# A two-layer graph attention kernel: one quarter of the attention weights read from its mirrored quarter

## The chip, the cores and the metric

The kernel runs on one core of a Trainium2 chip. A core has five engines that run side by side, each with its own queue in program order: TensorE (PE, matrix products), VectorE (DVE), ScalarE (ACT), GpSimd (POOL) and SyncE (SP, which here issues almost all transfers). Sixteen DMA engines move data between the core's memory SBUF and DRAM. The metric is the device time of one execution in microseconds (us), as the median of several runs; lower is better.

## The reference, cut to what matters

The input is 16 graphs (batches) of 1024 nodes with 256 features, and a symmetric 0/1 adjacency matrix with ones on its diagonal. Two layers follow each other. Layer 0 is attention with 8 heads of 32 features and an MLP; layer 1 is a single-head graph attention. The change touches the attention of layer 0:

```
normed = layer_norm(x, gamma1, beta1)
qkv    = normed.reshape(b_, n_, H, HD).transpose(0, 2, 1, 3)
scores = einsum('bhqd,bhkd->bhqk', qkv, qkv) * scale
masked = where(adj > 0, scores, -inf)
attn   = softmax(masked, axis=-1)
out    = einsum('bhqk,bhkd->bhqd', attn, qkv)
x      = x + out
y      = layer_norm(x, gamma2, beta2)
x      = x + gelu(y @ W1 + b1) @ W2 + b2
```

Queries, keys and values are the same matrix, and the mask is symmetric, so before the division by the row sum the weight of query q on key k equals that of query k on key q.

## The kernel before, in words

`fast_path` builds one straight program for all 16 batches. (A second path, `general_path`, runs only if a bound checked at the end is broken; it does not run here.)

*Attention of a batch* (`attention`, L966). The 8 heads make two groups `g` of four; the 1024 queries make two halves `qh` of 512; the keys make eight tiles `kt` of 128. A unit is one (qh, g, kt), 32 in a batch. `scores` (L971) lets PE form the scores of four heads in two PSUM tiles (L987), lets DVE add the mask to each (L1000, one 128x1024 instruction for two heads), and lets ACT take the exponential of each head with a running sum over the queries (L1007). Since weights are symmetric, that sum over the queries of a half is one half of a row sum. `weigh` (L1017) then multiplies the values with the weights into one PSUM tile of 128x512 for the group and half (L1022), one unit later: `go_on` (L1062) stands after the scores of the next unit. When a tile is complete it is copied (L1031), turned by PE and scaled by the inverted row sums (`finish`, L951; `invert`, L1038), and added to the layer's input by POOL (L964).

*The dense work of a batch* (`rest`, L1100) is the MLP and layer 1, cut into pieces of about 1.75 us of PE: `expand` (ph, L1158), `contract` (po, L1179), then projections and the attention of layer 1 (`weights`, lg, L1252, with DVE steps L1267 and L1272; `attend`, pa, L1291). It runs one batch behind the attention: while batch b does its attention, the pieces of batch b-1 fill PE between the units.

*Masks.* `turn_masks` (L889) loads four tiles of the adjacency matrix, converts them on DVE (L592) and transposes them by DMA; `compare_masks` (L909) checks on POOL (L917) and DVE (L924) that the mask is symmetric. `prologue` (L774) loads and normalises the next batch's input, with POOL forming the values (L814, L815).

*The order of the work* is set when the program is built. Each stream (attention, dense work, masks, next batch's prologue and so on, L1421 to L1483) yields a place on a common axis on which batch b's attention reaches from b to b+1; a loop (L1487) always advances the stream that is furthest behind. Beside this runs a clock of planned PE time (`clock`); `defer` (L757) puts an instruction into the queues once that clock has advanced by a given number of us. What results is one fixed order on each engine. Buffers come from pools of a fixed number; an engine waits in its queue until the buffer and the inputs of its next instruction are ready.

Pools that the change touches: `mqp` (converted masks, 2 buffers), `midp` (hidden layers and layer-1 matrices, 3), `ep` (exponentials, 6), `denp` (row sums).

Of the kernel before, what the change touches and what calls it, by code (L numbers as in the profile page):

```python
# [495 lines left out]
def fast_path(  # L496
# [49 lines left out]
    mqp = pool("mqp", 2)  # L546
# [3 lines left out]
    midp = pool("midp", 3)  # L550
    ep = pool("ep", 6)
# [222 lines left out]
    def prologue(b, st):  # L774
# [61 lines left out]
        if b == 0:  # L836

            tiles = [midp.tile([P, 2, N], I32, tag="mid", name=f"adj_0_{i}") for i in range(2)]
            adjs = [tiles[t // 2][:, t % 2] for t in range(TPH)]
            mqs = st["mq", 0] = mqp.tile([P, TPH, N], FP8, tag="mq", name="mq_0_0")  # L840
            m = st[0] = mkp.tile([P, NT // 2, QW, 2], FP8, tag="mk", name="mk_0_0")
            pairs = m.rearrange("p m q r -> p m (q r)").bitcast(BF16)

            def fetch(t):
                nc.sync.dma_start(adjs[t], rows(adj, 0, t))

            def convert(t):
                nc.vector.tensor_scalar(
                    mqs[:, t], adjs[t], 0.0, NEG8, op0=ALU.is_le, op1=ALU.mult, saturate=False
                )  # L850
                nc.sync.dma_start_transpose(pairs[:, :, t * P : (t + 1) * P], mqs[:, t].bitcast(BF16))

            for f, i in ((load, 0), (fetch, 0), (load, 1), (fetch, 1), (fetch, 2), (fetch, 3), (load, 2), (load, 3)):
                f(i)
            measure(0, "a")
            measure(1, "a")
            rectify(0)
            convert(0)
            rectify(1)
            measure(0, "b")  # L860
            convert(1)
            measure(1, "b")
            value(0)
            turn(0)
            convert(2)
            value(1)
            turn(1)
            convert(3)
            for f in (lambda i: measure(i, "a"), rectify):
                for i in (2, 3):  # L870
                    f(i)
            yield
            measure(2, "b")
            value(2)
            yield
            measure(3, "b")
            value(3)
            yield
            for i in (2, 3):
                turns.append((1, lambda i=i: turn(i)))  # L880
                yield
            return
# [83 lines left out]
    def attention(b, st):  # L966
        va, kT = st["va"], st["kT"]
        den = denp.tile([P, NQH, NT, H], F32, tag="den", name=f"den_{b}")


        def scores(qh, g, kt):  # L971
# [24 lines left out]
            for i in range(2):  # L996
# [7 lines left out]
                def weights(e=e, masked=masked, i=i):  # L1004
                    for j in range(2):
                        n = g * GH + 2 * i + j
                        nc.scalar.activation(  # L1007
                            e[:, j], masked[:, j], AF.Exp, scale=SCALE, accum_out=den[:, qh, kt, n : n + 1]
                        )
# [4 lines left out]

        acc, os, rl = {}, {}, {}

        def weigh(qh, g, kt, es):  # L1017
            if kt == 0:
                acc[g, qh] = pso.tile([P, QW], F32, tag="o", name=f"o_{b}_{g}_{qh}")
            o = acc[g, qh]  # L1020
            for j in range(GH):
# [4 lines left out]
                    start=(kt == 0),  # L1026
                    stop=(kt == NT - 1),
                )
            if kt == NT - 1:
# [8 lines left out]
        def invert(qh, g):  # L1038
            r = smallp.tile([P, TPH, GH], F32, tag="rl", name=f"rl_{b}_{g}_{qh}")
            ts, hs_ = slice(qh * TPH, (qh + 1) * TPH), slice(g * GH, (g + 1) * GH)  # L1040

            def f():
                nc.vector.tensor_tensor(r, den[:, 0, ts, hs_], den[:, 1, ts, hs_], op=ALU.add)
                nc.vector.reciprocal(r, r)

            rl[g, qh] = r, defer(2.5, f)

        units = [(qh, g, kt) for qh in range(NQH) for g in range(NG) for kt in range(NT)]
        for u in units:
# [4 lines left out]
            scored.append((weigh, (*u, es)))  # L1054
            qh, g, kt = u
            if qh == NQH - 1 and kt % TPH == TPH - 1:
                invert(kt // TPH, g)
                if kt < NT - 1:
                    close(kt // TPH, g)
            yield  # L1060
# [39 lines left out]
    def rest(b, st, tails):  # L1100
# [55 lines left out]
        def expand(c):  # L1156
            yield from wait_for(turn, c)
            hid = midp.tile([P, FC, CW], F32, tag="mid", name=f"hid_{b}_{c}")  # L1158
# [190 lines left out]
        fT = st["fT"] = midp.tile([P, DC, N], F32, tag="mid", name=f"fT_{b}")  # L1349
# [5 lines left out]
        uT = midp.tile([P, DC, N], F32, tag="mid", name=f"uT_{b}")  # L1355
# [64 lines left out]

    def stream_a():  # L1421
        for b in range(B):
            yield from spread(attention(b, states[b]), 32, b, b + 1)
        yield from spread(close_attention(), 4, B, B + .1)

    def stream_b():
        for b in range(B):
            done = 0.0
            place = b + 0.99
            yield place  # L1430
            for us, others in states[b]["rest"]:
# [8 lines left out]
                elif others:  # L1440
                    place = max(place, b + 1 + done / B_US)
                yield place
        for us, _ in tails[B]():
            clock[0] += us
            yield B + 1

    def stream_p():
        for b in range(B):
            for c in range(2):
                yield b + 0.91 + 0.025 * c  # L1450
                prepare(b, states[b], c)
            yield b + 0.96
# [12 lines left out]
    def stream_m():  # L1465
        for b in range(B):
            for qh in range(b == 0, NQH):
                yield from spread(turn_masks(b, qh, states[b]), 5, b + 0.5 * qh - 0.27, b + 0.5 * qh - 0.07)

    def stream_k():  # L1470
        for b in range(B):
            for qh in range(NQH):
                yield from spread(
                    compare_masks(b, qh, states[b]), TPH * (qh + 1), b + 0.5 * qh + 0.02, b + 0.5 * qh + 0.2
                )
# [85 lines left out]
```

## Time and profile before

| what | value |
|---|---|
| three runs | 3424.79, 3426.13, 3426.3 us; median 3426.13 |
| profiled execution | 3422.06 us, of which the profile's span is 3420.3 us |
| busy: PE / DVE / ACT / POOL | 98% / 82% / 60% / 26% of the span |
| DMA engines, main queue | 15.8% busy, 137.56 MB |
| clock granted to PE | 0.999 |
| first batch's attention | up to about 141 us |
| attention of batches 1 to 15 | about 141 us to 3262 us, 208 to 211 us each |
| end, dense work of the last batch alone | about 3262 us to 3420 us |

The times of the table's last rows are read from the first mask addition of each batch. In the profile's lines "L1000" is a line of the kernel, "out<-in" are the program's names of tiles, "xN" the number of instructions; behind the bar stand the busy time in us, the mean of one in ns, and the idle time of the engine just before them with what ended it. PE's records count twice the matmuls that the code names: each matmul of these 4-byte numbers appears as two.

### The profile page before, as it was taken

To read this page: it belongs to the slowest core of one execution; us is meant where nothing else is said; L and a number is where in the kernel's file an instruction comes from. 1 tells how busy PE (TensorE), PEld (TensorE's weight loads), DVE (VectorE), ACT (ScalarE), POOL (GpSimd) and SP (SyncE) were. 2 spreads that over 40 slices of the span, in tenths; PEclk is the share of its full clock that TensorE was granted. 3 is DMA by queue.
4 is the path that set the end of the run, shared out by engine and by line. 5 is a ranking of instruction groups with operands and counts; after the bars stand their busy time and mean duration, and the time that the engine had idled before them with its cause. 6 is when DMAs were issued, how large, how long until landed. Compare 5 with 4: busy or idle time off the path is not lost. (4 is left out here: it accounts for less than half of the span.)

```text
span 3420.3 us, 114618 instructions
## 1 busy us (share of the span) xinstructions
PE 3356.2 (98%) x49790; PEld 1603.4 (47%) x49790; DVE 2799.1 (82%) x5427; ACT 2061.6 (60%) x5192; POOL 880.6 (26%) x1038
## 2 busy tenths in 40 slices
PE   6899999999999999999999999999999999999998
PEld 1244444444444444444444444444444444444477
DVE  6788888888888978888888887888879788897854
ACT  6665666656566565666656656666665655666532
POOL 3422232222323222232222312223222232321120
PEclk9999999999999999999999999999999999999999
DMA  4111202112011121111211112120211211111000
GB/s 135 45 39 40 57 17 54 39 47 56 20 46 39 48 54 34 40 31 48 54 39 48 25 50 45 42 56 18 52 39 48 55 26 40 39 48 42 8 19 14
DMA packets 157471, 145.22 MB, mean 42 GB/s; under 512 B 81056, under 2 KB 116256, under 8 KB 156960
## 3 DMA queue, kind: packets, MB, share of 16 engines
q1 hardware_dynamic: 156672, 137.56, 15.8%
q8 instruction: 392, 6.42, 0.8%
q14 instruction: 119, 0.97, 0.1%
q10 hardware_dynamic: 288, 0.26, 0.0%
HBM read 104.21 MB, written 16.78 MB: 35 GB/s over the span
## 5 line engine op out<-in xcount | busy, mean ns | idle before, releaser
L1007 ACT ACTIVATE e<-e 128x512 f32<-128x512 f32 x1984 | 1224.8, 619 | 960.5 <-DVE e L1000 958.1
L1000 DVE TENSOR_TENSOR e<-s,mk 128x1024 f32<-128x1024 f32 x992 | 1168.1, 1218 | 195.2 <-PE s L987 192.7
L987 PE MATMUL s<-kT 32*64 32x512 f32 x8192 | 579.5, 615 | 1.1 <-DVE e L1000 0.9
L1022 PE MATMUL o<-e,va 128*32 128x512 f32 x4096 | 557.5, 606 | 1.3 <-ACT e L1007 1.3
L572 PE MATMUL lg<-fT,uT 128*32 128x256 f32 x7680 | 454.1, 379 | 0.0
L572 PE MATMUL pa<-gw,e 128*32 128x258 f32 x7552 | 453.3, 380 | 0.0
L572 PE MATMUL ph<-yT,w 128*32 128x256 f32 x7808 | 451.0, 379 | 0.0
L572 PE MATMUL po<-w,hid 128*32 128x256 f32 x7680 | 438.9, 379 | 0.0
L1007 ACT ACTIVATION_READ_ACCUMULATOR e<-e 128x1 f32 x1984 | 371.2, 187 | 0.0
L572 PEld LDWEIGHTS ph<-yT,w 128*32 128x32 f32 x7808 | 255.5, 110 | 213.0 <-issue 55.7
L572 PEld LDWEIGHTS lg<-fT,uT 128*32 128x32 f32 x7680 | 257.3, 110 | 200.5 <-issue 43.3
L572 PEld LDWEIGHTS pa<-gw,e 128*32 128x32 f32 x7552 | 252.3, 110 | 206.6 <-issue 56.5
L572 PEld LDWEIGHTS po<-w,hid 128*32 128x32 f32 x7680 | 249.6, 110 | 209.6 <-issue 62.8
L1022 PEld LDWEIGHTS o<-e,va 128*32 128x32 f32 x4096 | 83.6, 108 | 424.6 <-issue 198.9
L1267 DVE SCALAR_TENSOR_TENSOR e<-lg,gw,mk 128x256 f32<-128x256 f32 x512 | 221.7, 474 | 64.2 <-PE lg L572 37.4
L1273 ACT ACTIVATE e<-e,shift 128x512 f32<-128x512 f32 x256 | 182.2, 715 | 141.5 <-DVE e L1272 103.8
L964 POOL TENSOR_TENSOR h<-h,ot 128x512 f32<-128x512 f32 x64 | 84.7, 1323 | 697.8 <-DVE ot L960 697.8
L917 POOL TENSOR_TENSOR odd<-mk,mq 128x512 bf16<-128x512 fp8e5 x192 | 233.3, 1216 | 100.2 <-DVE uneven L924 100.2
L1170 DVE TENSOR_TENSOR hid<-ph,b1c 128x512 f32<-128x512 f32 x256 | 173.6, 683 | 77.8 <-PE ph L572 67.8
L1272 DVE SCALAR_TENSOR_TENSOR e<-e 128x512 f32<-128x512 f32 x256 | 209.5, 818 | 8.8
L987 PEld LDWEIGHTS s<-kT 32*64 32x64 f32 x8192 | 122.7, 130 | 161.0 <-issue 105.0
L744 POOL TENSOR_TENSOR rs_c<-ve_c,mhalf 128x2 f32<-128x2 f32 x64 | 44.5, 695 | 477.4 <-DVE ve_c L742 378.1
(135 smaller groups left out, 3477.0 us busy)
## 6 DMA issues: line engine op xcount, KB each, us to landing
adj<-in_adj_dram SPq DMA_DIRECT2D x248, 256.0 KB, 3.6
h<-in_x_dram SPq DMA_DIRECT2D x64, 256.0 KB, 4.0
xb<-in_x_dram SPq DMA_DIRECT2D x128, 128.0 KB, 2.3
out_dram<-z SPq DMA_DIRECT2D x128, 128.0 KB, 1.7
adj<-in_adj_dram SPq DMA_DIRECT2D x4, 512.0 KB, 7.0
mk<-mq SPq DMA_TRANSPOSE x128, 3.8
w<-in_L_gnn_W_dram SPq DMA_DIRECT2D x2, 1024.0 KB, 8.7
wo<-in_L_gnn_W_dram SPq DMA_DIRECT2D x2, 256.0 KB, 9.8
```

Source lines behind the costliest of these rows:

```text
L572: nc.tensor.matmul(out[c : c + HD], lhsT[:, c : c + HD], rhs, start=start, stop=stop)
L744: nc.gpsimd.tensor_tensor(rs, ve, mhalf[:, :nt], op=ALU.pow)
L917: nc.gpsimd.tensor_tensor(odd.rearrange("p (u v x) -> p u v x", u=2, v=2), key.rearrange("p (u v x) -> p u v x", u=2, v=2), query.rearrang ...
L964: nc.gpsimd.tensor_add(ho, ho, ot.rearrange("p t j d -> p t (j d)"))
L987: nc.tensor.matmul(sc[j // 2][c : c + P // 2, j % 2, :], kT[r, g, kt * P + c : kt * P + c + P // 2], kT[r, g, qs], start=j >= by_pe, stop= ...
L1000: nc.vector.tensor_tensor(e, masked, mb, op=ALU.add)
L1007: nc.scalar.activation(e[:, j], masked[:, j], AF.Exp, scale=SCALE, accum_out=den[:, qh, kt, n : n + 1])
L1022: nc.tensor.matmul(o[j * HD : (j + 1) * HD, :], va[:, kt, (g * GH + j) * HD : (g * GH + j + 1) * HD], es[j // 2][:, j % 2, :], start=(kt = ...
L1170: nc.vector.tensor_tensor(hid[:, f0 : f0 + 2, :], ph, b1c[:, f0 : f0 + 2].unsqueeze(2).to_broadcast([P, 2, CW]), op=ALU.add,)
L1267: nc.vector.scalar_tensor_tensor(e[:, j, :], lg[:, j, :], gw[:, kt, D : D + 1], st[c // 2][:, kt // 2, qs, kt % 2], op0=ALU.add, op1=ALU.add,)
L1272: nc.vector.scalar_tensor_tensor(e, e, ALPHA, e, op0=ALU.mult, op1=ALU.max)
L1273: ready = defer(2.5, lambda: nc.scalar.activation(e, e, AF.Exp, bias=shift))
```

## The change

Batches 1 to 15 no longer compute the quarter of queries 512 to 1023 on keys 0 to 511 (qh 1, kt 0 to 3). Its weights are those of queries 0 to 511 on keys 512 to 1023 (qh 0, kt 4 to 7), mirrored. Batch 0 is as before, apart from its row sums' layout.

- The units of a batch are now 16 of the first half, keys 4, 0, 5, 1, 6, 2, 7, 3 for each group, and then 8 of the second half, keys 4 to 7 only.
- `mirror`, for each of the 8 units that are the source: when its exponentials are there, DVE turns them in blocks of 32x32 into one tile `x` (1 MB, one buffer), two instructions of 128x1024. Then SP issues four writes of 256 KB, one for each 32 partitions, to a scratch in DRAM, where the blocks' place stands for their new partitions.
- `fetch`, 16 a batch: SP issues a read of 512 KB from the scratch into one of the two halves of a tile `em`. The next fetch into a half waits until PE and POOL have read it.
- `weigh_mirrored`, 16 a batch, two in each of the 8 later units: four matmuls of 256 columns add to the same PSUM tile as the unit's own. POOL adds up the 8 blocks of two fetches to row sums in five additions; DVE reduces these to the inverse (in `invert`).
- The pools `mqp`, `midp` and `ep` give up buffers (2 to 1, 3 to one for each of three tags, 6 to 4) for the new tiles.
- The order is moved: units have widths (1 for the first 16, 1.15 for the last 8), the dense work of a batch starts at 1.08 batches behind in place of 0.99 and only when the first half of the queries is finished (now at the last unit), and masks are turned and compared at other places.

```diff
-    mqp = pool("mqp", 2)
+    mqp = pool("mqp", 1)
...
-    midp = pool("midp", 3)
-    ep = pool("ep", 6)
+    midp = pool("midp", 1)
+    ep = pool("ep", 4)
+    xp = pool("xp", 1)
+    dramp = pool("dramp", 2, space=bass.MemoryType.DRAM)
...
                         nc.scalar.activation(
-                            e[:, j], masked[:, j], AF.Exp, scale=SCALE, accum_out=den[:, qh, kt, n : n + 1]
+                            e[:, j], masked[:, j], AF.Exp, scale=SCALE,
+                            accum_out=sums[kt // TPH, g][:, n, kt % TPH, qh : qh + 1],
                         )
...
+        def mirror(g, kt, es):
+            x = xp.tile([P, NT // 2 * GH, GH, HD], F32, tag="x", name=f"x_{b}_{g}_{kt}")
+            if g not in blocks:
+                blocks[g] = dramp.tile([NT // 2 * GH, NT // 2 * GH, HD, P], F32, tag=f"blocks{g}", name=f"blocks_{b}_{g}")
+
+            def turn(i):
+                nc.vector.transpose(
+                    x[:, :, 2 * i : 2 * i + 2, :].rearrange("p c h j -> p h c j"),
+                    es[i].rearrange("p h (c i) -> p h c i", i=HD),
+                )
+
+            def write():
+                for a in range(GH):
+                    nc.sync.dma_start(
+                        blocks[g][(kt - TPH) * GH + a].rearrange("c i e -> i c e"),
+                        x[a * HD : (a + 1) * HD].rearrange("p c h j -> p c (h j)"),
+                    )
+
+            defer(1.5, lambda: turn(0))
+            defer(3.5, lambda: turn(1))
+            defer(5.5, write)
+
+        def fetch(k):
+            g, t, half = k // (2 * TPH), k // 2 % TPH, k % 2
+            if k == 0:
+                blocks["e"] = midp.tile([P, 2, 2 * GH, P], F32, tag="mid0", name=f"em_{b}")
+            nc.sync.dma_start(
+                blocks["e"][:, half],
+                blocks[g][half * 2 * GH : (half + 1) * 2 * GH, t * GH : (t + 1) * GH].rearrange(
+                    "k b i e -> (b i) k e"
+                ),
+            )
+
+        def weigh_mirrored(k):
+            g, t, half = k // (2 * TPH), k // 2 % TPH, k % 2
+            e = blocks["e"][:, half]
+            if t == half == 0:
+                acc[g, 1] = pso.tile([P, QW], F32, tag="o", name=f"o_{b}_{g}_1")
+            o = acc[g, 1]
+            for j in range(GH):
+                nc.tensor.matmul(
+                    o[j * HD : (j + 1) * HD, half * CW : (half + 1) * CW],
+                    va[:, t, (g * GH + j) * HD : (g * GH + j + 1) * HD],
+                    e[:, :, j * HD : (j + 1) * HD],
+                    start=t == half == 0,
+                    stop=False,
+                )
+            add = lambda out, p, q: nc.gpsimd.tensor_tensor(out, p, q, op=ALU.add)
+            if half == 0:
+                if t == 0:
+                    blocks["rows", g] = denp.tile([P, TPH, P], F32, tag="rows", bufs=1, name=f"rows_{b}_{g}")
+                blocks["part"] = denp.tile([P, GH, P], F32, tag="part", bufs=1, name=f"part_{b}_{g}_{t}")
+                add(blocks["part"], e[:, :GH], e[:, GH:])
+            else:
+                part = blocks["part"]
+                add(part, part, e[:, :GH])
+                add(part, part, e[:, GH:])
+                add(part[:, :2], part[:, :2], part[:, 2:])
+                add(blocks["rows", g][:, t], part[:, 0], part[:, 1])
+            clock[0] += 0.45
+            if k + 2 < 2 * TPH * NG:
+                defer(2.5 + 2.0 * half, lambda: fetch(k + 2))
+            if t == TPH - 1 and half == 1:
+                invert(0, g)
+                close(0, g)
...
+        keys = list(range(NT))
+        if mirrored:
+            keys = [kt for pair in zip(keys[TPH:], keys[:TPH]) for kt in pair]
+        units = [(0, g, kt) for g in range(NG) for kt in keys]
+        keys = list(range(TPH if mirrored else 0, NT))
+        units += [(1, g, kt) for g in range(NG) for kt in keys]
...
+            if qh == 0:
+                if kt >= TPH:
+                    mirror(g, kt, es)
+                if n == NG * NT - 1:
+                    defer(2.0, lambda: fetch(0))
+                    defer(2.2, lambda: fetch(1))
+                yield 1.0
+                continue
+            if last:
+                invert(1, g)
+            widths = (0.5, 0.4, 0.25) if first else (0.3, 0.5, 0.35)
+            yield widths[0]
+            weigh_mirrored(k)
+            yield widths[1]
+            weigh_mirrored(k + 1)
+            k += 2
+            yield widths[2]
...
+    def starts(b):
+        return b + (1.08 if b else 0.99)
...
-                    place = max(place, b + 1 + done / B_US)
+                    place = max(place, start + length * done / B_US)
```

## The prediction

> **What bounds the kernel now.** I read the busy table first, then the groups, then the TensorE (PE) timeline of a few units in a steady batch, then the busy times of one whole batch, and last the landing times of the transfers.
>
> ```profile
> span 3420.3 us, 114618 instructions
> PE 3356.2 (98%) x49790; PEld 1603.4 (47%) x49790; DVE 2799.1 (82%) x5427; ACT 2061.6 (60%) x5192; POOL 880.6 (26%) x1038
> ...
> L1007 ACT ACTIVATE e<-e 128x512 f32<-128x512 f32 x1984 | 1224.8, 619 | 960.5 <-DVE e L1000 958.1
> L1000 DVE TENSOR_TENSOR e<-s,mk 128x1024 f32<-128x1024 f32 x992 | 1168.1, 1218 | 195.2 <-PE s L987 192.7
> L987 PE MATMUL s<-kT 32*64 32x512 f32 x8192 | 579.5, 615 | 1.1 <-DVE e L1000 0.9
> L964 POOL TENSOR_TENSOR h<-h,ot 128x512 f32<-128x512 f32 x64 | 84.7, 1323 | 697.8 <-DVE ot L960 697.8
> L1272 DVE SCALAR_TENSOR_TENSOR e<-e 128x512 f32<-128x512 f32 x256 | 209.5, 818 | 8.8
> ```
>
> PE is busy 98% of the span and its matmul groups show next to no idle time in front of them (1.1 us for 8192 score matmuls). A busy PE need not be a full one, so the timeline:
>
> ```profile
> 1047.38 3.64 PE L572 MATMUL ph<-yT,w 128*32 128x256 f32 x64
> 1050.94 1.11 PE L987 MATMUL s<-kT 32*64 32x512 f32 x16
> 1051.99 1.06 PE L1022 MATMUL o<-e,va 128*32 128x512 f32 x8
> 1052.87 5.36 PE L572 MATMUL po<-w,hid 128*32 128x256 f32 x96
> 1058.16 0.66 PE L1219 MATMUL ptf<-ident,ft 128*128 128x128 f32 x4
> 1058.75 1.11 PE L987 MATMUL s<-kT 32*64 32x512 f32 x16
> ```
>
> Columns: start, length. From start to start the scores of a unit cost 1.05 us (1051.99 - 1050.94), its weighing 0.88, 32 records of the dense layers 1.77 (5.29 for 96), four transposes 0.59. Summed over the instructions of a batch (32 units, 288 groups of four quarter matmuls at 0.44, 8 at 0.87, 16 sets of transposes) this is 205 us; a steady batch takes 208.5:
>
> ```profile
> 1395.90:1604.40 208.50, 206.66 (x3188) 96.78 (x3184) 176.13 (x341) 129.01 (x325) 54.90 (x64) 1.00 0.16 43
> ```
>
> (length; PE, weight loads, VectorE (DVE), ScalarE (ACT), GpSimd (POOL) busy; granted clock; DMA share; GB/s). So PE bounds the 15 steady batches, with only 3.4 us of a batch not explained by its work. DVE, at 176 us (84%), is the next.
>
> **The change part by part.** Batch 0 keeps all units; batches 1 to 15 do 24 units instead of 32.
>
> *Removed.* 8 score sets a batch: 8 x 1.05 = 8.4 us of PE, on the path. With them 16 mask adds (16 x 1.218 = 19.5 us of DVE) and 32 exponentials with their accumulator reads (32 x 0.806 = 25.8 us of ACT). ACT waits 958 us for the adds already, so its share is worth nothing.
>
> *PE, exchanged.* 8 weigh sets of 512 columns (8 x 0.88 = 7.0) become 16 of 256 columns. In the tile shape of the dense layers, also 256 wide, four cost 0.44: 7.1 us. Their moving operand is read in runs of 32; no row shows that, the strided weights of the dense layers run at the same pace, and I take 0.
>
> *DVE, added.* 16 turns of 128x1024 replace the 16 adds. No row shows a turn. Rows bound it: 0.84 us by the rate of the mask conversion (420 ns for 512), 1.63 by the statistics (407 ns for 256); I take the add's 1.22, as many elements in one instruction, and the middle. So the batch sum is unchanged but for two reductions (about 0.68 each, as a 128x512 reduce), yet the place changes: all turns lie in the first 16 units. By the built order of the changed kernel those units hold 228 DVE instructions, 129.7 us by row means (adds 39.0, turns 19.5, hidden-layer adds 10.9, statistics 17.7, the rest small). Row means overlap: a batch of before has 193 us of them in 176 busy, a factor 0.91, so about 118.5 us (113 and 124 at the ends), against 122.2 of PE in the same units. Nearly two full engines. The first two units are the worst, about 19.5 us of DVE against 14.7 of PE: late by 5 us, more than the 4 or so between the end of two adds and the next scores. I take 1.2 us of PE idle a batch; ends 0 and 5. The last 8 units: DVE 65.1 x 0.91 = 59 against PE 74.6.
>
> A turn waits for two exponentials, and in DVE's order the next adds stand behind it, and PE's next scores behind those. From the start of a unit's first add the exponentials end after 1.2 + 1.6 = 2.8 us and 4.4 us; the order puts 2.8 to 5.7 us and 5.0 to 6.8 us of DVE work ahead of the two turns. Covered, except where a Gelu (1.9 us plus two table loads of 1.3) falls between; inside the 0 to 5 above.
>
> *SP queue and transfers.* A batch gets 32 writes (256 KB) and 16 fetches (512 KB): 48 issues at 0.4 us, 19 us of an idle queue, and 16 MB. The main queue's 137.56 MB took 15.8% of the engines; 240 MB more adds about 28%. Volume does not bind; latency may. The single turn tile must be written out before the next turn, two units or 15 us later: about 3 us to the second turn's end, 1.6 for four issues, landing as below: 10 us. Covered. Queued behind these on SP are mask loads, mask transposes and output stores; masks have a lead of some 30 us.
>
> ```profile
> adj<-in_adj_dram SPq DMA_DIRECT2D x248, 256.0 KB, 3.6
> xb<-in_x_dram SPq DMA_DIRECT2D x128, 128.0 KB, 2.3
> ...
> w<-in_L_gnn_W_dram SPq DMA_DIRECT2D x2, 1024.0 KB, 8.7
> ```
>
> *The fetch loop (added wait).* Each half of the fetched tile is used once per unit of the last 8, about 9.3 us. It is free when PE (0.4) and POOL's reading adds (1.3, or 2.6 for the second half) are done, then issue 0.4, then landing. Landing lies between 3.6 (half the bytes) and 8.7 us (twice the bytes, queued behind others); I take 5.0. Loop: 8.4 of 9.3 us. Behind a late fetch wait PE's mirrored matmuls and, behind those, its next scores. I take 0.5 us a batch; ends 0 and 22 (8.7 gives 2.8 us x 8).
>
> *POOL.* 40 adds a batch: 24 x 1.3 + 8 x 0.78 + 8 x 0.48 (an estimate, on the line through the two others) = 42 us, so 97 of some 203 instead of 55, nearly all in the last 8 units: 52.5 of 74.6 us. In the first of them the order also has two mask comparisons (1.2) and four adds of the next batch's values: 10.7 us against PE's 8.6, so its buffer comes free 2 us late. I take 1.0 us; ends 0 and 3.
>
> POOL also slows DVE. DVE operations with two inputs in SBUF have long outliers:
>
> ```profile
> L1272 DVE SCALAR_TENSOR_TENSOR e<-e x256: 691/692/1695, 252.9 to 3403.0; 128x512 f32<-128x512 f32 x128
> ...
> L924 DVE TENSOR_TENSOR uneven<-uneven,odd x192: 408/416/1416, 34.3 to 3207.2; 128x256 int32<-128x256 int32 x192
> ```
>
> (min/median/max). The means, 818 and 538, lie 0.13 and 0.12 us over the medians with POOL busy 26%; at 70% that is 0.34 each: 12 and 6 of them, and 10 smaller ones at 0.1, make about 7 us of DVE a batch, 4.5 more than now, inside its 15 us of room. [...]
>
> *Edges.* The last batch's first rows are now finished only with its last unit; about 8% of the previous batch's dense work is left to cover that. I take 3 us once; ends 0 and 8.
>
> **Sum.** Per batch -8.4 + 1.2 + 0.5 + 1.0 = -5.7; fifteen times -85; with the edge -82. The profiled execution took 3422.06 us, so 3340; the median of the runs shown, 3426.13, lies 4 above, so the forecast is 3344 us.
>
> **Rivals.** All are given as medians.
> - *All hidden:* PE stays packed as now: 3426 - 125 = 3301. For it: in before's last 8 units DVE has 53.9 us of row means against 50.7 of PE without PE idling. Chance 0.20.
> [...]
> - *The fetch loop decides (slower).* At a landing of 6 us the loop equals the unit; each further us costs 8 x 15 = 120 us. The 82 us are gone at 6.7; at 7.5, the quicker of the two 1 MB loads, 3344 + 180 = 3524. For it: packets half the length, reads scattered over 16 blocks. Against: 1024 packets on 16 engines are few. 0.14.
> - *A turn takes twice an add:* +19.5 us of DVE in the first stage, 138 against 122 of PE, of which some 4 run over into the second: +12 x 15, 3524. No row is that slow. 0.12.
> - *The removed scores weren't the bound:* 3426. Against it the packed timeline. 0.03.
>
> The forecast itself: 0.37, its own range 3315 to 3390. A measurement tells 0.2% (7 us) from no change. Faster: 0.37 + 0.20 + 0.11 = 0.68; same 0.03 + 0.03 = 0.06; slower 0.26 (the two slow rivals). The range, 3298 to 3470, leaves out the upper part of those two, under 0.2.
>
> **What the profile after would show.** A steady batch of about 203 us; 8192 score records down to about 6270; a turn's row near 1.2 us; POOL near 1510 us; landing of the fetches 4 to 6 us; waits of PE's mirrored matmuls for the fetched tile of a few tens of us in all. I am wrong if these waits are some hundreds of us, if a turn takes over 1.7 us, or if the scores wait long for the adds in the first 16 units.

## The result

The changed kernel took 3724.73 us (median of four, 3721.07 to 3728.12), the kernel before 3425.68 beside it: a ratio of 1.0873 (95% interval 1.0854 to 1.0892), 299 us slower. The forecast was 3344, its range 3298 to 3470.

The page of the changed kernel:

```profile
span 3726.3 us, 113449 instructions
...
PE 3368.4 (90%) x48710; PEld 1646.5 (44%) x48710; DVE 2891.1 (78%) x5457; ACT 1766.4 (47%) x4232; POOL 1517.1 (41%) x1638
```

The granted clock, the mean over the span, fell from 0.999 to 0.969. That splits the 306 us between the two profiled spans. PE's idle time (span less busy) rose from 64 to 358 us: +294. The time lost to the clock, estimated as span times (1 - clock), rose from 3 to 116: +112. PE's busy time less that loss fell from 3353 to 3253: -100. So the removed products are there; idle time and the lower clock behind it are four times as large.

Groups by line and shape, the DMA queue and the DMA issues of the changed kernel (L1030 turn, L994 scores, L1064 mirrored products, L1050 fetch, L1037 write):

```profile
L994 PE MATMUL s<-kT 32*64 32x512 f32 x6272 | 456.2, 618 | 2.1 <-DVE e L1007 0.5
L1030 DVE STREAM_TRANSPOSE x<-e 128x1024 f32<-128x1024 f32 x240 | 294.7, 1232 | 9.0 <-issue 5.1 <-ACT e L1014 1.6 <-DMA blocks<-x 1.5
L1064 PE MATMUL o<-em,va 128*32 128x256 f32 x1920 | 162.6, 412 | 208.8 <-DMA em<-blocks 149.6 <-DVE os L1106 59.0
```

```profile
q1 hardware_dynamic: 659712, 389.26, 42.1%
...
blocks<-x SPq DMA_DIRECT2D x480, 256.0 KB, 4.4
em<-blocks SPq DMA_DIRECT2D x240, 512.0 KB, 4.5
```

The number of score records, the turn, GpSimd's busy time, the queue's share and the landing are all where the forecast put them. The 208.8 us of idle time before L1064 are not. PE's waits, the longest four:

```profile
PE o L1064 <- DMA em<-blocks: 149.6, 66, 4.3
PE o L1064 <- DVE os L1106: 59.0, 30, 3.2
PE ph L574 <- DVE yT L1257: 33.8, 14, 3.2
PE lg L574 <- DVE z L1424: 28.1, 14, 2.3
```

A steady batch in windows: the whole of it, its first 26 us (about three units), and the second stage, which is its last 96 us:

```profile
1503.80:1732.00 228.20, 208.03 (x3141) 99.60 (x3140) 182.17 (x343) 109.18 (x260) 97.53 (x105) 0.97 0.46 112
1503.80:1530.00 26.20, 21.39 (x309) 9.63 (x312) 24.88 (x49) 8.99 (x24) 9.55 (x12) 1.00 0.28 72
1636.00:1732.00 96.00, 82.84 (x1208) 38.59 (x1196) 64.93 (x112) 36.13 (x92) 57.83 (x55) 0.93 0.45 116
```

This batch takes 228 us instead of 208.5. PE idles 13 us in the second stage at a clock of 0.93, and 5 us in the first three units, where VectorE is busy 95%. Three places are to be explained: the fetched tile, the accumulator behind `os`, and the first units.

**Why a fetch is late.** A half of the fetched tile can be filled again when PE and GpSimd have read it. GpSimd in the first units of the second stage (start, length):

```profile
1643.51 1.28 POOL L1071 TENSOR_TENSOR part<-em 128x512 f32<-128x512 f32 x1
1644.74 1.60 POOL L919 TENSOR_TENSOR odd<-mk,mq 128x512 bf16<-128x512 fp8e5 x1
1646.31 2.89 POOL L1071 TENSOR_TENSOR part<-part,em 128x512 f32<-128x512 f32 x2
...
1650.50 1.16 POOL L919 TENSOR_TENSOR odd<-mk,mq 128x512 bf16<-128x512 fp8e5 x1
1652.86 0.83 POOL L816 TENSOR_TENSOR nrm<-nrm,g 128x256 f32<-128x256 f32 x1 [1.20 <-DVE nrm L750]
...
1656.41 1.72 POOL L1071 TENSOR_TENSOR part<-em 128x512 f32<-128x512 f32 x1
1658.09 2.27 POOL L919 TENSOR_TENSOR odd<-mk,mq 128x512 bf16<-128x512 fp8e5 x2
1660.32 3.13 POOL L1071 TENSOR_TENSOR part<-part,em 128x512 f32<-128x512 f32 x2
```

Between the sums stand mask comparisons (L919) and the next batch's values (L816), one of which waits for VectorE. From the records, averaged over the 15 batches, GpSimd's last read of the halves that fetches 2 to 6 fill ends 2.5 to 8.3 us after PE's; these fetches then start within 0.2 us. Later in the stage GpSimd is in time, and SyncE is not (its queue, then PE's):

```profile
1663.48 3.12 SPq L1050 DMA_DIRECT2D em<-blocks  x2
1675.02 0.36 SPq L1431 DMA_DIRECT2D out_dram<-z  x1
1675.50 1.40 SPq L1050 DMA_DIRECT2D em<-blocks  x2
```

```profile
1673.85 3.67 PE L574 MATMUL pa<-gw,e 128*32 128x258 f32 x64
1679.76 0.64 PE L1064 MATMUL o<-em,va 128*32 128x256 f32 x8 [2.24 <-DMA em<-blocks]
```

An output store stood first in SyncE's queue until VectorE had its rows, at 1675.02. The fetch behind it fills the half that PE's product of 1667.78 used and that GpSimd's additions left at 1670.05; it was issued at 1675.50, and PE waited for it until 1679.76. On average fetches 7, 9, 12, 13 and 15 are issued 3.3 to 5.4 us after their half is free, behind such a store or behind a mask load that waits for the mask conversion.

### The profile page after: what moved, and what is told of

It reads as the page before. It is cut to its first block, busy times and chain, and to the rows that moved or that the text cites. A ratio compares the mean times of both kernels' runs of the same rounds, so it can differ in the third digit from the quotient of the medians.

```text
span 3726.3 us, 113449 instructions
## 1 busy us (share of the span) xinstructions
PE 3368.4 (90%) x48710; PEld 1646.5 (44%) x48710; DVE 2891.1 (78%) x5457; ACT 1766.4 (47%) x4232; POOL 1517.1 (41%) x1638
## 5 line engine op out<-in xcount | busy, mean ns | idle before, releaser
L1014 ACT ACTIVATE e<-e 128x512 f32<-128x512 f32 x1504 | 928.3, 618 | 1057.3 <-DVE e L1007 1054.7
L1007 DVE TENSOR_TENSOR e<-s,mk 128x1024 f32<-128x1024 f32 x752 | 884.7, 1216 | 90.3 <-PE s L994 85.2
L574 PE MATMUL lg<-fT,uT 128*32 128x256 f32 x7648 | 502.5, 408 | 28.1 <-DVE z L1424 28.1
L574 PE MATMUL ph<-yT,w 128*32 128x256 f32 x7680 | 465.0, 390 | 33.8 <-DVE yT L1257 33.8
L994 PE MATMUL s<-kT 32*64 32x512 f32 x6272 | 456.2, 618 | 2.1 <-DVE e L1007 0.5
L1097 PE MATMUL o<-e,va 128*32 128x512 f32 x3136 | 442.9, 607 | 1.9 <-ACT e L1014 1.8
L1071 POOL TENSOR_TENSOR part<-part,em 128x512 f32<-128x512 f32 x240 | 323.3, 1347 | 275.5 <-DMA em<-blocks 265.9
L1064 PE MATMUL o<-em,va 128*32 128x256 f32 x1920 | 162.6, 412 | 208.8 <-DMA em<-blocks 149.6
L1030 DVE STREAM_TRANSPOSE x<-e 128x1024 f32<-128x1024 f32 x240 | 294.7, 1232 | 9.0 <-issue 5.1
L1014 ACT ACTIVATION_READ_ACCUMULATOR e<-e 128x1 f32 x1504 | 280.7, 187 | 0.0
L1382 DVE SCALAR_TENSOR_TENSOR e<-e 128x512 f32<-128x512 f32 x256 | 246.0, 961 | 8.8
L919 POOL TENSOR_TENSOR odd<-mk,mq 128x512 bf16<-128x512 fp8e5 x192 | 228.7, 1198 | 44.2 <-DVE uneven L926 44.2
```

The source lines that it names most:

```text
L574: nc.tensor.matmul(out[c : c + HD], lhsT[:, c : c + HD], rhs, start=start, stop=stop)
L919: nc.gpsimd.tensor_tensor(odd.rearrange("p (u v x) -> p u v x", u=2, v=2), key.rearrange("p (u v x) -> p u v x", u=2, v=2), query.rearrang ...
L994: nc.tensor.matmul(sc[j // 2][c : c + P // 2, j % 2, :], kT[r, g, kt * P + c : kt * P + c + P // 2], kT[r, g, qs], start=j >= by_pe, stop= ...
L1007: nc.vector.tensor_tensor(e, masked, mb, op=ALU.add)
L1014: nc.scalar.activation(e[:, j], masked[:, j], AF.Exp, scale=SCALE, accum_out=sums[kt // TPH, g][:, n, kt % TPH, qh : qh + 1],)
L1030: nc.vector.transpose(x[:, :, 2 * i : 2 * i + 2, :].rearrange("p c h j -> p h c j"), es[i].rearrange("p h (c i) -> p h c i", i=HD),)
```

## The experiments

Idle is the span less PE's busy time, "clock loss" the span times (1 - granted clock). Single executions unless an interval is given.

| run | us | idle | clock loss |
|---|---|---|---|
| before | 3425.68 | 64 | 3 |
| the change | 3724.73 | 358 | 116 |
| e1 fetch once (work left out) | 3518 | 235 | 32 |
| e2 fetches from GpSimd's queue | 3706 | 358 | 96 |
| e3 stores issued later | 3650 | 305 | 91 |
| e4 no sums (work left out) | 3579 | 267 | 57 |
| e5 no turns (work left out) | 3656 | 331 | 84 |
| e6 before, with the small pools | 3424 | 65 | 7 |
| e7 two fetched tiles | 3532 | 245 | 32 |
| e8 = e7, copies on ScalarE | 3535 | 238 | 60 |
| e11 = e7, late products | 3480 | 205 | 21 |
| e12 = e11, other key order | 3502 | 227 | 53 |
| e13 = e11, tail first | 3504 | 218 | 35 |
| e14 = e11, both | 3492 | 231 | 31 |
| e15 = e11, narrow second stage | 3546 | 237 | 67 |
| e16 = e15, values later | 3548 | 242 | 60 |
| e17 = e11, no turns (work left out) | 3431 | 182 | 24 |
| e18 = e11, later start | 3400 | 132 | 17 |
| e20 = e18, no turns (work left out) | 3315 | 87 | 20 |
| e21 = the change, later start | 3560 | 252 | 46 |

### What the fetch loop costs, and which queue makes it late

```diff
-            if k + 2 < 2 * TPH * NG:
-                defer(2.5 + 2.0 * half, lambda: fetch(k + 2))
```

> Only the first two halves of each batch's mirrored weights are fetched; the other 14 fetches of a batch are left out and the mirrored products use the first two halves again (so the output is not the reference's). Starting point 3725 us. Theory 'fetch loop': the units that wait for fetched weights carry 4.3, 4.0, 4.5, 5.0 and 1.4 us of excess over PE's own work (batch 7), 19 us a batch, 15 batches: 3725 - 288 = about 3437 us (3400 to 3470), with PE's granted clock back near 0.99 in the last eight units. Rival 'VectorE or GpSimd sets the pace of the last eight units anyway': less than 60 us gained, above 3665. Rival 'first units': what remains over 3340 stands in the first three units of a batch, 8.5 us each.

3518 us, 207 less: the direction of the fetch-loop theory, but 80 us short of its 288. The waits for the accumulator (59.5 us) and for yT (32) stayed. So without any refetch the change is still 95 us slower than before: the fetch loop isn't all.

```diff
-            nc.sync.dma_start(
+            nc.gpsimd.dma_start(
                 blocks["e"][:, half],
...
-                defer(2.5 + 2.0 * half, lambda: fetch(k + 2))
+                fetch(k + 2)
```

> The fetches are issued from GpSimd's queue, right behind its own additions that free the buffer, instead of from SyncE's. Theory A (SyncE's order: the fetch stands behind output stores and mask loads that wait for VectorE): the lateness of fetches 7, 9, 12, 13 and 15 (3.3 to 5.4 us each from buffer free to issue) goes; excess of the units that use them was 4.0 + 4.5 + 5.0 + 1.4 = 15 us a batch: 3725 - 225 = 3500 us (3470 to 3560). Theory B (GpSimd is late with its additions, so the buffer comes free late): only that lateness remains, it carries all, and the time stays above 3665 us. Both true by the shares read: 3500, with the 4.3 us of the unit of fetches 4 and 5 left.

3705.59 us, ratio to before 1.0825 (1.0806 to 1.0843): 19 us gained where theory A alone expected 225. PE's waits for the fetched tile fell from 149.6 to 97.8 us, but an issue holds GpSimd for 0.9 us (240 of them), and a fetch that waits for PE now holds GpSimd's own queue (82.4 us in 46 waits, the longest 4.7). A as the only cause is out; the run moves the cost rather than isolating B.

```diff
-                nc.sync.dma_start(rows(out, b, t), z)
+                defer(5.0, lambda: nc.sync.dma_start(rows(out, b, t), z))
```

> The output store's DMA is issued 5 us (of the planned clock) later than before, when its rows are already computed; nothing else is moved. Theory A: the stores no longer hold SyncE's queue, the mask loads still do; about half of the 15 us a batch: 3725 - 110 = 3615 us (3560 to 3680). Theory B or a rival in which the landing alone decides: 3725, within 20 us.

3650 us, 75 less, inside A's range. (The late store may read its tile after other rows have been given it, so only the time counts here.) PE's waits for the tile fell to 87.6 us. The stores ahead of the fetches are a real part.

```diff
-            add = lambda out, p, q: nc.gpsimd.tensor_tensor(out, p, q, op=ALU.add)
...
-                add(blocks["rows", g][:, t], part[:, 0], part[:, 1])
+            if half == 0 and t == 0:
+                blocks["rows", g] = denp.tile([P, TPH, P], F32, tag="rows", bufs=1, name=f"rows_{b}_{g}")
+                nc.gpsimd.memset(blocks["rows", g], 1.0)
```

> GpSimd's five additions a unit, which sum the mirrored weights for the denominators, are left out (the output is not the reference's); the fetched tile is then freed by PE alone. Theory B: the 4.3 us of the unit of fetches 4 and 5 go, and part of the 4.0 behind it: 3725 - 65 to 125 = 3600 to 3660 us. Theory A alone: SyncE's lateness remains and nothing changes by more than 40 us (above 3685). A third theory, that the additions slow VectorE's two-input operations at the shared memory: VectorE's busy time falls by over 60 us (4 us a batch).

3579 us, 146 less, past theory B's 125: the late release by GpSimd is a real part as well. PE's waits for the tile fell to 73.9 us, not far below the 87.6 of e3, so the runs don't rank the two queues: in this one VectorE gains too, and how much of the 146 us is due to that isn't shown. VectorE's busy time fell from 2891.1 to 2822.9 us, 4.5 us a batch; where the additions slow it, at the memory or elsewhere, isn't shown. One of its operations with two inputs in SBUF, a layer-1 step, in the changed kernel and then in the run without the sums (busy us, mean ns):

```profile
L1382 DVE SCALAR_TENSOR_TENSOR e<-e 128x512 f32<-128x512 f32 x256 | 246.0, 961 | 8.8
```

```profile
L1373 DVE SCALAR_TENSOR_TENSOR e<-e 128x512 f32<-128x512 f32 x256 | 198.6, 776 | 8.8
```

This row makes up 47 of the 68 us. Another 14 come from the mask conversion, which has one input (473 ns a piece in the changed kernel, 420 without the sums and in the kernel before).

Both queues make the one tile late; e7 takes away what both act on, by a second tile, so that a fetch may start a unit earlier:

```diff
+            if k == 2:
+                blocks["e", 1] = xp.tile([P, 2, 2 * GH, P], F32, tag="x", name=f"em_{b}_1")
...
-                blocks["e"][:, half],
+                blocks["e", t % 2][:, half],
...
-            if k + 2 < 2 * TPH * NG:
-                defer(2.5 + 2.0 * half, lambda: fetch(k + 2))
+            if k + 4 < 2 * TPH * NG:
+                defer(2.5 + 2.0 * half, lambda: fetch(k + 4))
```

> The mirrored weights are fetched into two tiles in turn (the second takes the place of the turns' tile, which is idle in the last eight units), so each fetch may start a unit (9.3 us) earlier. Theory 'late buffer' (GpSimd, PE and SyncE's order free the single buffer too late for a landing of 4.5 us): the waits for fetched weights go and the time comes down to that of the kernel that fetches only once, 3518 us (3500 to 3560). Rival 'transfers themselves are too slow' (16 MB a batch against the engines' share): under 60 us gained, above 3665.

3532.16 us, ratio to before 1.0316 (1.0299 to 1.0333): 193 us back, with every transfer, sum and turn in place. The rival that the transfers are too slow is out. PE's first waits now:

```profile
PE o L1066 <- DVE os L1108: 59.5, 30, 4.9
PE ph L574 <- DVE yT L1261: 33.7, 14, 3.2
```

### The pools and the turns

e6 is the kernel before with `mqp` of one tile and `ep` of four.

> The kernel before, with the two smaller pools of the change alone (four exponential tiles instead of six, one mask code tile instead of two). Theory 'the change pays for its room': over 20 us slower than 3422. Theory of the fetch loop and VectorE: within 7 us of 3422.

3424 us: these two smaller pools cost nothing by themselves in the order of the kernel before. The third pool, `midp`, was not tried alone.

```diff
-            defer(1.5, lambda: turn(0))
-            defer(3.5, lambda: turn(1))
```

(The writes then send a constant tile.)

> The 16 turns of a batch are left out; a constant tile is written to the scratch in their place (the output is not the reference's). VectorE loses 16 x 1.23 = 19.7 us a batch, all in the first 16 units. Theory 'VectorE is full in the first units': the excess of the first three units, 8.5 us a batch (2.7 and 5.8 in most batches), goes for the most part: 3725 - 90 to 125 = 3600 to 3635 us. Rival 'the first units were late for another reason' (SyncE's stores, the previous batch's rest): less than 30 us gained, above 3695.

3656 us, 69 less, between the two theories' bounds. PE's waits for yT stayed at 33.7 us, so these are not the turns' doing; what went were the waits for z (28.1 us) and three rows of waits for gw (10.9, 6.9 and 3.5 us), while those for the fetched tile rose from 149.6 to 167.7 us.

### The accumulator

There is one PSUM tile for the weighed sums. The first mirrored products of a group need it after VectorE has copied the previous sums, and that copy stands behind two mask additions (2.35 us). e8 lets ScalarE copy:

```diff
-                nc.vector.tensor_copy(c, o)
+                nc.scalar.copy(c, o)
...
-            (nc.vector.tensor_copy if t % 2 else nc.scalar.copy)(gw
+            nc.scalar.copy(gw
```

> As the kernel with two tiles, and the copies of the weighed sums (682 ns, 4 a batch) and of the node values (424 ns, 4 a batch on VectorE) go to ScalarE. Theory 'VectorE's queue is what remains': PE's gaps before the mirrored products (0.9 + 2.9 us in a batch) and before the node values' stage (0.8 + 0.5 + 0.6) that end with those copies go, 3 to 5 us a batch with the half clock behind them: 45 to 80 us below the kernel with two tiles, some 3440 to 3475. Rival 'the copy waits for PE either way' or ScalarE's own queue is no better: within 20 us of the kernel with two tiles.

3535 us: nothing gained. ScalarE's exponentials, which stand ahead of the copy in its queue, wait for the same additions (1061 us in all), and PE now waits 63.5 us for ScalarE's copy. e11 leaves the copy and puts the products later in the unit:

```diff
-            widths = (0.5, 0.4, 0.25) if first else (0.3, 0.5, 0.35)
+            widths = (0.85, 0.2, 0.1) if first else (0.3, 0.5, 0.35)
```

> Two tiles for the fetched weights, and in the first unit of each group in the second stage the mirrored products are placed near the unit's end (0.85 of its width instead of 0.5). They need the accumulator that VectorE's copy of the previous sums frees, and that copy stands behind two mask additions (2.35 us). Theory 'VectorE's queue ahead of the copy': the gaps of 0.9 and 2.9 us before the mirrored products and the half clock behind the second (3.41 us at 0.5, 1.7 us lost) go: 3532 - 15 x 5.5 = 3450 us (3435 to 3480). Rival 'the wait only moves to the next product or to the next scores': above 3510.

3480 us, 52 less than e7 and at the upper edge of the expected range; the wait for `os` fell from 59.5 to 19.6 us.

### The first units of a batch

Five runs tested the reading that VectorE is too dense there: other key order (`zip(keys[:TPH], keys[TPH:])`, with the two later fetches of a batch's start moved 2.5 us behind it), part of the previous tail ahead of `expand(0)`, and a plan with less dense work in the second stage.

> As the kernel with late products, and the keys of a group go 0, 4, 1, 5, ... instead of 4, 0, 5, 1, ..., so that the first turns of a batch fall into its second unit. Theory 'VectorE is full in the first units by the turns': 1 to 3 us a batch less excess there, 15 to 45 us below the kernel with late products. Rival 'the previous batch's last dense rows fill VectorE there, the turns add to it wherever they stand': within 15 us.

> As the kernel with late products, and two pieces of the previous batch's last rows are placed between the transposes that VectorE turns into the hidden layer's input and the hidden layer itself, for which PE waited 2.35 us a batch (and about 0.4 to 1.5 us for the sums' buffer). Theory 'PE waits there only because nothing else is placed ahead': 2 to 4 us a batch, 30 to 60 us below the kernel with late products. Rival 'VectorE's backlog is the length of the wait and meets the next PE group': within 15 us.

> Both of the last two changes. If they act on separate waits their gains add up: 45 to 105 us below the kernel with late products, which would be 3350 to 3410 us and below the kernel before (3423). If both only shift one backlog of VectorE: no more than the better of the two.

3502, 3504 and 3492 us: each 12 to 23 us worse than e11 (12 is little more than the 7 us between executions of the changed kernel). Under the other key order the wait for yT grew to 65.5 us; with the tail first the hidden layer waited as long (36.5 us) for ScalarE's z instead.

```diff
-    WIDTH = NG * NT + NG * TPH * 1.15
+    WIDTH = NG * NT + NG * TPH * 0.8
...
-            widths = (0.85, 0.2, 0.1) if first else (0.3, 0.5, 0.35)
+            widths = (0.55, 0.15, 0.1) if first else (0.2, 0.35, 0.25)
```

> As the kernel with late products, and the units of the second stage get a width of 0.8 instead of 1.15 in the plan, so that about 0.8 us more of dense work stands in each unit of the first stage (5.4 to about 6.2 us) and 1.1 us less in each of the second. Theory 'VectorE is too dense in the first stage': the first units' gaps (1.5 + 2.35 us a batch) shrink by half or more: 20 to 50 us below the kernel with late products (3480), 3430 to 3460. Rival 'the first units wait for the rest of the batch before, wherever the density lies', or the second stage now runs out of time for its fetches: 3480 or more.

> As the kernel with the new widths, and the next batch's values are prepared 0.1 of a batch (some 21 us) later, so that VectorE's statistics and normalisations leave the first stage. Theory 'density of VectorE in the first stage': another 10 to 30 us. Rival 'GpSimd's additions are late again behind these values': slower than the kernel with the new widths.

3546 and 3548 us: 65 and 68 worse; in e16 PE again waits 27 us for fetches and 33.7 for yT. So the wait for yT did not move with this thinning. Since the waits for fetches came back with it, the two runs don't price density alone.

> As the kernel with late products, without VectorE's turns: GpSimd sets the turns' tile to a constant instead (the output is not the reference's). It prices the turns' 19.7 us a batch of VectorE once the fetch loop is out of the way. Theory 'the turns fill VectorE in the first stage': the gaps of the first units and of the node values (1.5 + 2.35 + 0.8 + 0.5 + 0.6 us a batch) go: 3480 - 60 to 90 = 3390 to 3420 us, below the kernel before. Rival 'these gaps are there without the turns': above 3455.

3431 us, 49 less than e11, and the wait for yT (33.8 us) is still there. For this wait, that pointed away from the turns to the order around it. The change starts a batch's dense layers at place 1.08 and no longer 0.99, since its first 512 rows are now finished only in its last units. In the built order the hidden layer then comes right behind the next scores and weighing, while in the kernel before two groups of layer-1 scores stood between. PE and VectorE of the changed kernel there:

```profile
1520.54 0.66 PE L1253 MATMUL pty<-ident,y 128*128 128x128 f32 x4
1521.29 2.22 PE L994 MATMUL s<-kT 32*64 32x512 f32 x16
1523.44 1.55 PE L1097 MATMUL o<-e,va 128*32 128x512 f32 x8
1527.34 3.04 PE L574 MATMUL ph<-yT,w 128*32 128x256 f32 x52 [2.35 <-DVE yT L1257]
```

```profile
1520.02 2.35 DVE L1007 TENSOR_TENSOR e<-s,mk 128x1024 f32<-128x1024 f32 x2
...
1526.74 0.99 DVE L1257 TENSOR_SCALAR yT<-pty,g,be 128x256 f32<-128x256 f32 x2
```

The transposes were done at 1521.2; VectorE came to them 5.5 us later. To bridge that, PE had the scores and the weighing of one unit. These usually take 1.05 and 0.88 us from start to start. Here they took 3.7, at a granted clock of 1.00, since they were themselves held up: the second half of the scores started when VectorE's second mask addition had ended (1522.4). In the kernel before, with 64 records of layer-1 scores between:

```profile
1384.46 0.66 PE L1143 MATMUL pty<-ident,y 128*128 128x128 f32 x4
...
1386.97 3.64 PE L572 MATMUL lg<-fT,uT 128*32 128x256 f32 x64
1390.43 1.91 PE L572 MATMUL ph<-yT,w 128*32 128x256 f32 x32
```

e18 starts the dense layers 0.03 of a batch later in the plan. The second edit only keeps the normalisation of the input where it was for these batches (1.08 - 0.08), so it is earlier as seen from the dense layers alone:

```diff
-        return b + (1.08 if b else 0.99)
+        return b + (1.11 if b else 0.99)
...
-            place = starts(b) - 0.08
+            place = b + (1.0 if b else 0.91)
```

> As the kernel with late products, and the dense layers of a batch start 0.03 of a batch later in the plan while its input is normalised 0.03 earlier: eight groups of the previous batch's scores (2 us of PE) then stand between the transposes and the hidden layer that waits for VectorE's result. Theory 'the first rows are finished late and the hidden layer follows without a lead': the wait of 2.35 us a batch goes: 3480 - 35 = 3445 us (3430 to 3460), the last batch's dense work 4 us later. Rival 'VectorE's backlog is met anyway by the next group': 3470 or more.

3399.74 us, ratio to before 0.9931 (0.9915 to 0.9948): 81 us less than e11, more than twice the expected, and faster than both kernels (0.7% below the one before). At the same place e18 has the order of the kernel before again (PE, then VectorE):

```profile
1384.26 0.66 PE L1257 MATMUL pty<-ident,y 128*128 128x128 f32 x4
...
1387.61 3.66 PE L574 MATMUL lg<-fT,uT 128*32 128x256 f32 x64
1391.09 1.91 PE L574 MATMUL ph<-yT,w 128*32 128x256 f32 x32
```

```profile
1387.99 0.99 DVE L1261 TENSOR_SCALAR yT<-pty,g,be 128x256 f32<-128x256 f32 x2
```

The page, one batch in windows with its first 26 us, and two of PE's waits that the change doesn't have:

```profile
span 3395.3 us, 113358 instructions
...
PE 3263.0 (96%) x48638; PEld 1629.6 (48%) x48638; DVE 2924.0 (86%) x5457; ACT 1769.3 (52%) x4232; POOL 1527.5 (45%) x1638
```

```profile
1367.50:1575.10 207.60, 201.83 (x3137) 98.48 (x3136) 185.10 (x343) 109.25 (x260) 97.89 (x104) 0.99 0.50 123
...
1367.50:1393.70 26.20, 24.72 (x385) 12.09 (x384) 25.23 (x51) 10.77 (x30) 11.48 (x12) 1.00 0.27 67
```

```profile
PE pg L574 <- ACT uT L1348: 27.6, 14, 2.3
...
PE pa L574 <- DVE e L1381: 19.9, 13, 1.8
```

VectorE is busy 25.23 of the first 26.2 us, even more than in the change (24.88), and PE idles 1.5 us instead of 4.8. With as much load and a lead, the idle time is a third. The lead is not all that changed: on average over batches 1 to 15 VectorE came to the transposes 5.2 us after their end in the change, 3.1 us in e18 and 1.5 before, so its backlog at this place is shorter too.

> The same without VectorE's turns (GpSimd sets their tile to a constant; the output is not the reference's). If turns and lead are separate costs, 49 us below the kernel with the later start: about 3396 us, below the kernel before; if the lead alone was what the turns filled, within 20 us of it.

3315 us, 84 less than e18: with the order mended, the turns' 19.7 us a batch of VectorE are the main price left. VectorE's load thus does cost time, about as much as the missing lead did in e11 (81 us).

> The changed kernel with the later start of the dense layers alone (one fetched tile, early products). With two tiles and late products the start was worth 81 us (3480 to 3400). If the missing lead is a cost of its own: 3725 - 81 = 3645 us (3620 to 3670). If the fetch loop's waits in the last eight units swallow it (what is saved in the first units is lost again at the fetches): above 3695.

3560.09 us, ratio to before 1.039 (1.0371 to 1.0408): the later start alone, in the changed kernel as it was, returns 165 us, twice what the first reading expected and outside both. PE's waits for the accumulator fall from 59.0 to 12.4 us and those for yT from 33.8 to 3.3, and those for the fetched tile shrink from 149.6 to 94.4:

```profile
PE o L1064 <- DMA em<-blocks: 94.4, 54, 4.5
...
PE o L1064 <- DVE os L1106: 12.4, 30, 3.2
```

The causes are therefore not additive: two tiles 193 and the start 165 alone, and with the late products (52 on top of two tiles) 325 together. That a later start also thins out what stands ahead of the copies and the fetches in the queues is what these rows suggest; which instruction it is was not isolated. The edit moves a batch's whole dense work against the attention, the masks and the next batch's input, and 0.03 is the only shift that was run: a fit of the orders that is good by chance is not excluded.

## Why the prediction was wrong

- **Rows, right.** Turn 1232 ns (1.22 taken), 6272 score records (6270), GpSimd 1517 us (1510), median landing 4.5 us (5.0, between 4 and 6; averaged over the batches, fetches 2 to 15 lie between 4.0 and 6.5), main queue 42% (15.8 + 28). VectorE's busy time in the first 16 units of the batch from 1503.8 us was 117.2 us (118.5).
- **GpSimd's slowing of VectorE, right, in part by luck.** 4.5 us a batch were estimated from the trace; without the sums VectorE's busy time is 68 us lower, 4.5 a batch. But 14 of the 68 us come from the mask conversion, which the estimate didn't have, and in e7, e11 and e18, which keep the sums and as many VectorE instructions, its busy time is another 33 to 76 us above that of the change, for a reason that these runs don't show. In the chances, 0.11 of "faster" and 0.03 of "same" stand for a gain mostly eaten, by a blocking of VectorE by GpSimd and by two dense stages; no run shows such a blocking, and what the runs showed of GpSimd's effect are these 4.5 us a batch.
- **The fetch loop, the step that failed first.** "Loop: 8.4 of 9.3 us ... I take 0.5 us a batch; ends 0 and 22." The landing was a little better than taken, but the half of the tile was not issued 0.4 us after its readers were done. The sum counted GpSimd's two reads and not its queue (5.9 us of comparisons, values and a wait between two units' sums), and it counted an issue on SyncE and not what stands ahead of it: the text named what is queued behind the fetches, never what the fetches are queued behind. Measured: 149.6 us of PE's waits, and 193 us by two tiles, 12.8 a batch. The rival "the fetch loop decides" has the right mechanism, but was priced by the landing, which needed to exceed 6.7 us; the delay came before the issue.
- **GpSimd's first unit, "1.0 us; ends 0 and 3".** The same step seen once: it priced one unit of lateness; the records show five fetches 2.5 to 8.3 us late. Leaving out the sums returned 146 us, some of it perhaps through VectorE.
- **VectorE's density, "1.2 us of PE idle a batch; ends 0 and 5".** PE idled 4.8 us in these units, near the upper end. But density alone does not set this: in e18 it is as high and PE idles 1.5. What the term left out is how much other work of PE stands between a result that VectorE owes and its use.
- **The edge, "I take 3 us once; ends 0 and 8".** "The last batch's first rows are now finished only with its last unit" was priced for the last batch. It holds for all fifteen: each batch's dense layers start from these rows, late and without a lead. Priced at 3 us, it is next to the fetch loop the dearest step: the later start alone returned 165 us, through the fetches and the accumulator too.
- **The accumulator, not priced at all.** The mirrored products open a new accumulation in the second stage with one PSUM tile for all: 59.0 us of waits, 52 us returned by placing them later.
- **The clock, not priced at all.** 116 us of the span's time are lost to it, by the estimate above, against 3 before; every stall of 2 us or more was booked at its own length.
- **The gain itself, right in kind and too large in size.** PE's busy time at full clock fell by 100 us, not 126. The records of the removed scores are all gone, so waits inside groups are the likely rest, since the trace counts waits this short as busy: the scores at 1521.29 took 2.22 us where 1.11 is usual, waiting for a mask addition, which is one of the forecast's own signs of being wrong. As an estimate from the trace's records, what groups of scores and weighing took beyond 1.11 and 1.06 us at full clock makes 42 us in the change and 20 before, 22 of the 26 that are missing. e18 shows the mechanism pays, 3400 against a forecast of 3344; with the turns left out 3315 was measured, near the rival "all hidden" at 3301.

## What to carry to other kernels

Of a transfer in a loop, price three times and not one: when its buffer is really released (the queue of its slowest reader), what stands ahead of it in the queue that issues it, and only then the landing. When a change makes a result available later, look in every iteration at who starts from it and how much other work stands between: here a lead was worth as much as the load that it had to bridge (81 and 84 us). Price a stall on PE that repeats with what follows it in the clock: here a stall of 2.24 us had 3.41 us at half clock behind it, by the estimate above another 1.7 us.

## What the runs showed of the hardware

In the changed kernel the granted clock fell from 1.00 to 0.50 after short stalls (the shortest 2.14 us). Its trace has 63 stretches at half clock: 57 of 3.41 us, five of 6.83, and one of 6.63 at the end of the span. All start on one grid of 3.41 us. Windows on this grid, PE's busy time right behind the length, the granted clock in the third column from the right:

```profile
1660.08:1663.50 3.42, 1.35 (x28) 0.83 (x32) 3.39 (x6) 0.00 (x0) 3.30 (x3) 1.00 0.43 130
1663.50:1666.91 3.41, 3.41 (x39) 1.69 (x35) 1.58 (x2) 3.37 (x10) 2.52 (x3) 0.50 0.55 154
1666.91:1670.32 3.41, 3.41 (x62) 1.96 (x55) 0.94 (x4) 0.68 (x2) 2.75 (x3) 1.00 0.56 159
...
1677.15:1680.56 3.41, 1.17 (x24) 0.54 (x20) 0.81 (x3) 0.51 (x1) 0.71 (x1) 1.00 1.03 289
1680.56:1683.98 3.42, 3.42 (x35) 1.62 (x25) 0.40 (x2) 0.00 (x0) 3.01 (x4) 0.50 0.02 6
1683.98:1687.39 3.41, 3.41 (x51) 1.41 (x53) 3.17 (x9) 0.72 (x1) 0.00 (x0) 1.00 0.13 38
```

A window in which PE was busy 1.35 or 1.17 us is followed by one at half clock, in which PE gets through 39 and 35 records where the next has 62 and 51. The stalls in them are gaps of 2.41 and 2.24 us. From 141 to 3560 us, on this grid: nine tenths of the 64 half-clock windows follow one in which PE was busy for at most 0.38 of it, and no window at full clock follows a share below 0.41. The kernel before has 2 stretches at half clock. Of the changed kernel's 90 idle gaps over 2 us about two thirds were followed by half clock. Which did, went by how they lay on the grid: of twelve gaps of 2.35 us, the seven that left PE busy for 0.31 to 0.35 of a window were, and the five that left it 0.42 or more of each window were not.

In e2 an issue of a 512 KB fetch from GpSimd's queue held that engine for 0.9 us (884 to 1067 ns over 240).
